# Cross-attention scores: the low 64 queries as one 64-row tile beside two groups of 32 high queries

## The chip, the core and the metric

The kernel runs on one core of a Trainium2 chip. The core has five engines with queues of their own: TensorE (PE in the profile; PEld are its weight loads), VectorE (DVE), ScalarE (ACT), GpSimd (POOL) and SyncE (SP, which issues most DMAs). The metric is the device time of one launch in microseconds, as the median of several runs. Before the change it is 1574.82 us (three runs, 1572.63 to 1575.15).

## What is computed

A block of cross-attention with a feed-forward network, in float32, for 128 sequences of 128 tokens with 256 features, 16 heads of 16 features. The part that matters here:

```python
q = (x @ Wq + bq).reshape(b, s, 16, 16).transpose(0, 2, 1, 3)
k = (ctx @ Wk + bk).reshape(b, s, 16, 16).transpose(0, 2, 1, 3)
v = (ctx @ Wv + bv).reshape(b, s, 16, 16).transpose(0, 2, 1, 3)
scores = jnp.einsum('bhqd,bhkd->bhqk', q, k) / 4.0
scores = jnp.where(j < i, scores, -1e30)       # query i sees the keys before it
attn = jax.nn.softmax(scores, axis=-1)
attn = attn.at[:, :, 0, :].set(0.0)
a = jnp.einsum('bhqk,bhkd->bhqd', attn, v).transpose(0, 2, 1, 3).reshape(b, s, 256)
x1 = layer_norm(x + a @ Wo + bo, ln1_g, ln1_b)
out = layer_norm(x1 + relu(x1 @ W1 + b1) @ W2 + b2, ln2_g, ln2_b)
```

The mask is causal: a query among the first 32 needs at most 32 keys, one among the first 64 at most 64, and so on.

## The kernel before

Two sequences are worked on together; there are 64 such pairs p. All orders are written by hand: the kernel turns the scheduler off (`manual_schedule`) for all five engines, so the text order of the calls is the order on each engine's queue. Pairs 0 and 1 are a start-up of their own (with `scores`, line 340, in which a tile is 32 rows by 64 queries); `third`, `fourth` and `fifth` are pairs 2 to 4; `step` (line 1227) is the regular step for p = 5 to 63, and `behind` (line 1303) finishes the last pairs. One step holds parts of several pairs: scores of p, context (`weigh`) and output projection of p - 2, hidden layer of p - 3, second FFN product of p - 4, and the projections for p + 1.

On TensorE a regular step is this row: `weigh(p-2)` (lines 572 and 583), `scores_both(p)` (line 412), `queries(p+1)` (271), `attention_out(p-2)` (603), `keys(p+1)` (271), `values(p)` (303), `second_by_seven(p-4)` (881), `hidden(p-3)` (790).

**Scores.** The 128 queries of a sequence fall into four groups of 32, g = 0 to 3, and group g is multiplied with its first `LENGTH[g]` = 32, 64, 96 or 128 keys. `group_scores` (line 402) makes one matmul for each chunk m of heads, sequence s and strip r of 32 rows: the stationary operand is 32 rows by 32 queries, the moving one 2 x `LENGTH[g]` columns (two heads), the output goes to the 32 PSUM partitions 32c with c = 2s + m, in a bank chosen by r. All four groups thus use 32x32 tiles of the array: 16 matmuls a group, 64 a step. `scores_both` (line 419) runs them in eight blocks of eight, alternating between strips 0, 1 and strips 2, 3.

**Softmax.** Groups 0 and 1 are called `LO`, groups 3 and 2 `HI`. For `LO`, DVE adds the mask from PSUM into the buffer `sm` (`masked`, line 432) and takes the maxima (`largest`, 439); ACT makes the exponentials head by head (`exponential_by_head`, 847), for `HI` straight out of PSUM; `divided` (455) sums on DVE, takes the reciprocal and multiplies on POOL (465); `turned` (485) transposes blocks of 32x32 on DVE into `tb`; `brought` (495) issues 16 DMAs on SP, which bring the pieces of `tb` to the partitions of `pT`, the moving operand of `weigh`. Two copies of `pT` alternate. Parts of it that no DMA writes are cleared once for each copy (`clear`, 369 and 370).

**Pads.** `empty(n)` (line 223) puts n NOP instructions into TensorE's queue. `second_by_seven` (872) computes the second FFN product as seven partial products of four matmuls each, with 11 or 10 pads spread over each product: 74 a step. `hidden` has three or four pads behind each matmul for p below 3. A float32 matmul call is four TensorE instructions (two weight loads and two matmuls), so a regular step has 172 calls, 74 pads and six waits: 768 instructions.

Of the kernel before, what the change touches and what calls it, by code (L numbers as in the profile page):

```python
# [19 lines left out]
def tile_cross_attention_block(  # L20
# [341 lines left out]
    for i in range(2):  # L362
        pT = const.tile([P, NS, 2, 12, 32], F32, tag=f"pT{i}", name=f"pT{i}")
        pTs.append(pT)

    def clear(p):

        pT = pTs[p % 2]
        nc.gpsimd.memset(pT[32:64, :, 0, 0:4, :], 0.0)
        nc.gpsimd.memset(pT[96:128, :, 0], 0.0)  # L370

    LENGTH = (32, 64, 96, 128)
    START = (2304, 1792, 1024, 0)
    COLUMN = (0, 384, 128, 512)
    WITHIN = (0, 32, 0, 96)
    HI, LO = (3, 2), (1, 0)

    def weights(p, g):

        st = states[p]  # L380
        if "sm" not in st:
            st["sm"] = wide(f"sm_{p}")
            st["nmx"] = small.tile([P, 4, HH], F32, tag="nmx", name=f"nmx_{p}")
            st["su"] = small.tile([P, 4, HH], F32, tag="su", name=f"su_{p}")
            st["rs"] = small.tile([P, 4, HH], F32, tag="rs", name=f"rs_{p}")
        n = LENGTH[g]
        return st["sm"][:, START[g] : START[g] + HH * n].rearrange("p (h j) -> p h j", j=n)

    def first_bank(p, g):
        return 4 if p > 3 and g < 2 else 0  # L390

    def place(g, r):
        return r if g > 1 else (r + 2) % 4

    def in_banks(p, g, at=slice(0, 4)):

        first = first_bank(p, g)
        return banks[:, first + at.start : first + at.stop].rearrange(
            "p r (e x) -> p (r e) x", e=2
        )[:, :, WITHIN[g] : WITHIN[g] + LENGTH[g]]  # L400

    def group_scores(p, g, strips=range(NS)):

        st = states[p]
        n = LENGTH[g]
        for m in range(KC):
            for s in range(2):
                c = 2 * s + m
                for r in strips:
                    strip, first = slice(32 * r, 32 * r + 32), s * P  # L410
                    out = banks[32 * c : 32 * c + 32, first_bank(p, g) + place(g, r)]
                    nc.tensor.matmul(  # L412
                        out.rearrange("p (e x) -> p e x", e=2)[:, :, WITHIN[g] : WITHIN[g] + n],
                        st["qT"][strip, m, first + 32 * g : first + 32 * g + 32],
                        st["kT"][strip, m, :, first : first + n],
                        start=True, stop=True,
                    )

    def scores_both(p):

        one, two = (0, 1), (2, 3)
        for strips, g in (
            (two, 1), (one, 3), (two, 0), (one, 2),
            (two, 3), (one, 1), (two, 2), (one, 0),
        ):
            group_scores(p, g, strips)

    def masked(p, g, at=slice(0, 4)):

        n = LENGTH[g]  # L430
        heads = slice(2 * at.start, 2 * at.stop)
        nc.vector.tensor_tensor(  # L432
            weights(p, g)[:, heads], in_banks(p, g, at),
            diag[:, None, P - n :].to_broadcast([P, 2 * (at.stop - at.start), n]), ALU.add,
        )

    def largest(p, g, src=None, heads=slice(0, HH)):
        src = weights(p, g) if src is None else src
        nc.vector.tensor_reduce(  # L439
            states[p]["nmx"][:, g, heads], src, AX.X, ALU.max, negate=True  # L440
        )

    def shifted(p, g):

        sm = weights(p, g)
        largest(p, g)
        nc.gpsimd.tensor_tensor(
            sm, sm, states[p]["nmx"][:, g, :, None].to_broadcast([P, HH, LENGTH[g]]), ALU.add
        )
# [5 lines left out]
    def divided(p, gs):  # L455

        st = states[p]
        su, rs = st["su"], st["rs"]
        for g in gs:
            nc.vector.tensor_reduce(su[:, g], weights(p, g), AX.X, ALU.add)  # L460
        part = slice(min(gs), max(gs) + 1)
        nc.vector.reciprocal(rs[:, part], su[:, part])
        for g in gs:
            sm = weights(p, g)
            nc.gpsimd.tensor_tensor(  # L465
                sm, sm, rs[:, g, :, None].to_broadcast([P, HH, LENGTH[g]]), ALU.mult
            )

    def turned(p, g):

        st = states[p]
        if "tb" not in st:
            st["tb"] = wide(f"tb_{p}").rearrange("p (j n) -> p j n", j=NS)
        tb, sm = st["tb"], weights(p, g)
        n = 128 if g < 2 else 256
        to = tb[:, :, COLUMN[g] : COLUMN[g] + n].rearrange("p j (n a) -> p n j a", a=32)
        if g == 0:
            to = to[:, :, 0::2]
            sm = sm.rearrange("p (r e) a -> p r e a", e=2)
        elif g == 1:  # L480
            sm = sm.rearrange("p (r e) (k a) -> p r (e k) a", e=2, a=32)
        else:
            to = to[:, :, : g + 1]
            sm = sm.rearrange("p h (j a) -> p h j a", a=32)
        nc.vector.transpose(to, sm)  # L485
# [75 lines left out]
    def weigh(p):  # L561
# [6 lines left out]
        for m in range(KC):  # L568
            for s in range(2):
                at = (m * 2 + s) * P  # L570
                for j in range(NS):
                    nc.tensor.matmul(  # L572
                        pc[32 * j : 32 * j + 32, at : at + HP],
                        st["vd"][:, s, 4 * m + j].rearrange("p e d -> p (e d)"),
                        pT[:, 2 * s + m, :, (j + 2) % 4, :] if new
                        else pT[:, 2 * s : 2 * s + 2, H + 2 * j + m, :],
                        start=True, stop=True,
                    )
            for s in range(2):
                at = (m * 2 + s) * P  # L580
                for e in range(2):
                    for j in range(NS):
                        nc.tensor.matmul(  # L583
                            pc[32 * j : 32 * j + 32, at + HP : at + P],
                            st["vz"][:, s, 4 * m + j, 2 * e : 2 * e + 2, :].rearrange(
                                "p e d -> p (e d)"
                            ),
                            pT[:, 2 * s + m, :, 4 + 2 * j + e, :] if new
                            else pT[:, 2 * s : 2 * s + 2, 4 * j + 2 * m + e, :],
                            start=(e == 0), stop=(e == 1),  # L590
                        )
# [187 lines left out]
    def hidden(p, fs, between=None):  # L779
# [3 lines left out]
        for f in fs[::2]:  # L783
# [4 lines left out]
            for i in range(2):  # L788
                for k in range(KC):
# [5 lines left out]
                    if p < 3:  # L795
                        empty(3 + (2 * f + 2 * i + k < 12))
# [42 lines left out]

    def exponential_by_head(p, gs, heads):  # L840

        st = states[p]
        for h in heads:
            for g in gs:
                sm = weights(p, g)
                src = in_banks(p, g)[:, h] if g > 1 else sm[:, h]
                nc.scalar.activation(  # L847
                    sm[:, h], src, AF.Exp, bias=st["nmx"][:, g, h : h + 1], scale=1.0
# [23 lines left out]
    def second_by_seven(p):  # L872
# [19 lines left out]
        product(py[:, :P], raw(0, 0), weights(0, 0), 11)  # L892
        product(pz[:, :P], raw(1, 0), weights(1, 0), 11)
        product(pz[:, 2 * P : 3 * P], raw(1, 1), lambda k: wt[:, 3, k], 11)
        product(py[:, 3 * P :], lambda k: hs[:, 0, k], lambda k: wt[:, 0, k], 11)
        product(py[:, 2 * P : 3 * P], lambda k: hs[:, 2, k], lambda k: wt[:, 2, k], 10)
        product(py[:, P : 2 * P], lambda k: hs[:, 1, k], lambda k: wt[:, 1, k], 10)
        product(pz[:, P : 2 * P], lambda k: hs[:, 3, k], weights(1, 1), 10)
# [36 lines left out]
    warm = bank("warm")  # L935
    for i in range(12):
# [135 lines left out]
    def low_scores(p):  # L1072
        for g in LO:
            group_scores(p, g)
# [7 lines left out]
    def third():  # L1082
# [20 lines left out]
        divided(p, (3,))  # L1103
# [6 lines left out]
        divided(p, (2,))  # L1110
# [3 lines left out]
        divided(p, LO)  # L1114
# [24 lines left out]
    def fourth():  # L1139
# [12 lines left out]
        divided(p, (3,))  # L1152
        powers(p, 2)
        second_sum(0)
        divided(p, (2,))
        weigh(p - 1)
        context(p - 1)
        for g in LO:
            group_scores(p, g)
# [15 lines left out]
        divided(p, LO)  # L1175
# [13 lines left out]
    def fifth():  # L1189
# [19 lines left out]
        divided(p, (3,))  # L1209
        for g in LO:  # L1210
            powers(p, g)
        divided(p, (2,))
        divided(p, LO)
# [5 lines left out]
        for g in (3, 2, 1, 0):  # L1219
# [7 lines left out]
    def step(p):  # L1227
# [23 lines left out]
        if p > 5:  # L1251
            exponential_by_head(p, LO, range(HH))
# [9 lines left out]
        if p == 5:  # L1262
            exponential_by_head(p, LO, range(HH))
# [4 lines left out]
        divided(p, (3,))  # L1268
        divided(p, (2,))
        divided(p, LO)  # L1270
# [15 lines left out]
        for g in (2, 1, 0):  # L1286
# [108 lines left out]
```

## Time and profile before

| | |
|---|---|
| median of three runs | 1574.82 us |
| the profiled execution | 1573.26 us, span of its instructions 1571.5 us |
| granted TensorE clock, mean | 0.998 |
| busy: PE, PEld, DVE, ACT, POOL | 98%, 88%, 77%, 69%, 78% |
| TensorE matmul records | 21894 |
| DMA engines, mean over the span | 120 GB/s |

The span goes from the first to the last instruction of the program. Starts of matmuls are observed; their ends are modelled, and matmuls are pipelined, so that the time between two starts says more than the length of a row. In the rows, "128*32 128x64 f32 x16" is a tile of 128 rows by 32 columns with 64 moving columns, 16 records; one matmul call leaves two records, one for each of its passes. NOPs stand under PEldq, the sequencer of TensorE.

### The profile page before, as it was taken

To read this page: it belongs to the slowest core of one execution; us is meant where nothing else is said; L and a number is where in the kernel's file an instruction comes from. 1 tells how busy PE (TensorE), PEld (TensorE's weight loads), DVE (VectorE), ACT (ScalarE), POOL (GpSimd) and SP (SyncE) were. 2 spreads that over 40 slices of the span, in tenths; PEclk is the share of its full clock that TensorE was granted. 3 is DMA by queue.
4 is the path that set the end of the run, shared out by engine and by line. 5 is a ranking of instruction groups with operands and counts; after the bars stand their busy time and mean duration, and the time that the engine had idled before them with its cause. 6 is when DMAs were issued, how large, how long until landed. Compare 5 with 4: busy or idle time off the path is not lost.

```text
span 1571.5 us, 59475 instructions
## 1 busy us (share of the span) xinstructions
PE 1545.9 (98%) x21894; PEld 1385.6 (88%) x21894; DVE 1208.4 (77%) x2548; ACT 1089.3 (69%) x3394; POOL 1226.3 (78%) x1364
## 2 busy tenths in 40 slices
PE   8998999999999999999999999999999999999997
PEld 6876989989989989899899899899899899899897
DVE  7876877778778778778778778778778787787764
ACT  5556767767767767767767677677677677677652
POOL 7865878887887788788788788788788778878874
PEclk9999999999999999999999999999999999999999
DMA  8445545545555555555455555455455455554331
GB/s 192 90 103 111 133 116 129 123 117 125 134 120 122 123 121 128 126 124 125 117 123 128 127 126 129 108 128 132 117 129 127 110 129 130 123 125 108 95 85 46
DMA packets 415329, 188.73 MB, mean 120 GB/s; under 512 B 282448, under 2 KB 390992, under 8 KB 415056
## 3 DMA queue, kind: packets, MB, share of 16 engines
q1 hardware_dynamic: 413152, 184.00, 50.9%
q8 instruction: 190, 3.11, 0.9%
q10 hardware_dynamic: 1904, 0.93, 0.3%
q14 instruction: 83, 0.68, 0.1%
HBM read 70.26 MB, written 33.29 MB: 66 GB/s over the span
## 4 chain that ended last, share of the span: by engine, by line
PE 94%; POOL 2%; DVE 2%; ACT 1%; DMA 1%; issue 1%; SPq 0%; ACTq 0%; POOLq 0%; DVEq 0%
PE banks L790 27%; PE banks L881 23%; PE banks L271 14%; PE banks L412 7%; PE banks L603 7%; PE banks L303 7%; PE banks L583 3%; PE banks L572 2%; PE banks L810 0%; ACT sm L847 0%; POOL sm L537 0%; DMA pT<-tb 0%; DMA c_first<-in_ctx_dram 0%; DMA x1T<-x1t 0%; PE banks L1346 0%
## 5 line engine op out<-in xcount | busy, mean ns | idle before, releaser
L790 PE MATMUL banks<-x1T,w 128*128 128x256 f32 x2048 | 453.9, 379 | 2.0 <-ACT kT L293 1.2
L790 PEld LDWEIGHTS banks<-x1T,w 128*128 128x128 f32 x2048 | 384.4, 190 | 53.0 <-ACT kT L293 1.6
L798 ACT ACTIVATE hT<-banks,b1e_c 128x256 f32<-128x256 f32 x504 | 211.2, 471 | 222.5 <-PE banks L790 222.3
L847 ACT ACTIVATE sm<-banks,nmx 128x128 f32<-128x128 f32 (+1 forms) x944 | 237.0, 402 | 154.4 <-POOL hS L869 141.8
L465 POOL TENSOR_TENSOR sm<-sm,rs 128x1024 f32<-128x1024 f32 x248 | 303.9, 1255 | 7.5 <-ACT vd L318 4.3
L432 DVE TENSOR_TENSOR sm<-banks,diag 128x256 f32<-128x256 f32 (+1 forms) x250 | 82.6, 371 | 211.4 <-PE banks L412 204.2
L623 POOL TENSOR_SCALAR ve<-mv 128x2 f32<-128x2 f32 x127 | 29.2, 230 | 250.9 <-DVE mv L617 250.4
L847 ACT ACTIVATE sm<-sm,nmx 128x64 f32<-128x64 f32 (+1 forms) x944 | 223.0, 422 | 0.0
L460 DVE TENSOR_REDUCE su<-sm 128x8 f32<-128x1024 f32 x248 | 192.3, 796 | 30.0 <-ACT sm L847 24.3
L485 DVE STREAM_TRANSPOSE tb<-sm 128x1024 f32<-128x1024 f32 x248 | 191.4, 811 | 0.2 <-POOL sm L465 0.2
L881 PE MATMUL banks<-wt,hS 128*128 128x128 f32 x1440 | 171.4, 275 | 2.2 <-POOL hS L868 2.2
L881 PEld LDWEIGHTS banks<-wt,hS 128*128 128x128 f32 x1440 | 165.9, 192 | 2.7 <-POOL hS L868 2.6
L439 DVE TENSOR_REDUCE nmx<-banks 128x4 f32<-128x512 f32 x236 | 136.3, 620 | 4.0
L412 PE MATMUL banks<-kT,qT 32*32 32x64 f32 (+3 forms) x7936 | 130.9, 305 | 2.3 <-issue 1.7
L271 PE MATMUL banks<-xT,wq 128*128 128x256 f32 x504 | 127.3, 396 | 3.5 <-DVE sm L432 3.5
L293 ACT ACTIVATE kT<-banks,bkh,half 128x256 f32<-128x256 f32 x252 | 125.5, 635 | 4.0 <-PE banks L271 3.9
L412 PEld LDWEIGHTS banks<-kT,qT 32*32 32x32 f32 x7936 | 108.8, 103 | 18.4 <-issue 3.5
L303 PE MATMUL banks<-wv,cT 128*128 128x256 f32 x512 | 121.1, 379 | 1.4 <-ACT sm L847 1.4
L603 PE MATMUL banks<-wo,cxT 128*128 128x256 f32 x512 | 122.0, 381 | 0.0
L271 PE MATMUL banks<-cT,wk 128*128 128x256 f32 x504 | 119.3, 379 | 1.6 <-DVE sm L432 1.6
L881 PEld LDWEIGHTS banks<-w,hT 128*128 128x128 f32 x960 | 116.5, 192 | 3.3
L881 PE MATMUL banks<-w,hT 128*128 128x128 f32 x960 | 117.2, 275 | 0.0
(137 smaller groups left out, 2916.9 us busy)
## 6 DMA issues: line engine op xcount, KB each, us to landing
pT<-tb SPq DMA_DIRECT2D x492, 96.0 KB, 2.2
pT<-tb SPq DMA_DIRECT2D x246, 80.0 KB, 2.1
x1t<-tbx SPq DMA_DIRECT2D x252, 64.0 KB, 3.1
x1T<-x1t SPq DMA_DIRECT2D x63, 256.0 KB, 2.8
out_dram<-t SPq DMA_DIRECT2D x63, 256.0 KB, 2.4
xb<-in_x_dram SPq DMA_DIRECT2D x124, 128.0 KB, 3.6
cb<-in_ctx_dram SPq DMA_DIRECT2D x124, 128.0 KB, 3.8
x<-in_x_dram SPq DMA_DIRECT2D x31, 512.0 KB, 4.8
```

What stands on the lines that cost most here:

```text
L271: nc.tensor.matmul(ps[:, m * TP : (m + 1) * TP], w[:, k, m * P : (m + 1) * P], src[:, k, :], start=(k == 0), stop=(k == KC - 1),)
L303: nc.tensor.matmul(pv[:, s * D : (s + 1) * D], st["cT"][:, k, s * P : (s + 1) * P], wv[:, k, :], start=(k == 0), stop=(k == KC - 1),)
L412: nc.tensor.matmul(out.rearrange("p (e x) -> p e x", e=2)[:, :, WITHIN[g] : WITHIN[g] + n], st["qT"][strip, m, first + 32 * g : first + 32 ...
L439: nc.vector.tensor_reduce(states[p]["nmx"][:, g, heads], src, AX.X, ALU.max, negate=True)
L460: nc.vector.tensor_reduce(su[:, g], weights(p, g), AX.X, ALU.add)
L465: nc.gpsimd.tensor_tensor(sm, sm, rs[:, g, :, None].to_broadcast([P, HH, LENGTH[g]]), ALU.mult)
L485: nc.vector.transpose(to, sm)
L603: nc.tensor.matmul(po[:, s * D : (s + 1) * D], cxT[:, k, s, :], wo[:, k, :], start=(k == 0), stop=(k == KC - 1),)
L790: nc.tensor.matmul(ph[:, i * TP : (i + 1) * TP].rearrange("p (s i a) -> p s i a", s=2, a=32), w1[:, k, (f + i) * P : (f + i + 1) * P], st[ ...
L798: nc.scalar.activation(st["hT"][:, f + i, :], ph[:, i * TP : (i + 1) * TP], AF.Relu, bias=(b1e_c if p else b1_c)[:, f + i : f + i + 1], sc ...
L847: nc.scalar.activation(sm[:, h], src, AF.Exp, bias=st["nmx"][:, g, h : h + 1], scale=1.0)
L881: nc.tensor.matmul(out, left(k), right(k), start=(k == 0), stop=(k == FC // 2 - 1))
```

## The change

The two low groups become one group of 64 queries with 64 keys. Its matmuls (`low_products`) have 32 rows by 64 queries as stationary operand and 2 x 64 moving columns, and write 64 PSUM partitions at once: 16 matmuls in place of 32, so 48 a step in place of 64. The high groups keep their 32x32 tiles. In `scores_both` the low matmuls go in four blocks of four between the high blocks. In the softmax the low group is now 16 heads of 64 keys for 64 queries of both sequences, 1024 elements in each partition where there were 512 and 256; each operation on it is one instruction in place of two, except the exponentials, which stay 16. The layout of `sm`, `tb` and `pT` changes with it, and the DMAs in `brought` with their sizes: 96 KB for j = 0 to 2, and 32 or 64 KB for j = 3, where there were 96, 80, 96 and 48. The masked-out piece of `pT` is cleared in one operation. The pads of `second_by_seven` become 20 or 19 a product, 138 a step, so that a regular step has 156 calls, 138 pads and six waits, again 768 instructions. The pads in `hidden` go.

```diff
-    LENGTH = (32, 64, 96, 128)
-    START = (2304, 1792, 1024, 0)
-    COLUMN = (0, 384, 128, 512)
-    WITHIN = (0, 32, 0, 96)
-    HI, LO = (3, 2), (1, 0)
+        nc.gpsimd.memset(pTs[p % 2][96:128], 0.0)
+    HEADS = (H, None, HH, HH)
+    LENGTH = (HP, None, 96, P)
+    START = (1792, None, 1024, 0)
+    WITHIN = (0, None, 0, 96)
+    COLUMN = (256, None, 0, 512)
...
+    def low_products(p, strips=range(NS), ms=range(KC)):
+        st = states[p]
+        bank0 = 4 if p > 3 else 0
+        for m in ms:
+            for s in range(2):
+                for r in strips:
+                    strip, first = slice(32 * r, 32 * r + 32), s * P
+                    nc.tensor.matmul(
+                        banks[s * HP : (s + 1) * HP, bank0 + (r + 2) % 4, m * P : (m + 1) * P].rearrange(
+                            "p (e j) -> p e j", e=2
+                        ),
+                        st["qT"][strip, m, first : first + HP],
+                        st["kT"][strip, m, :, first : first + HP],
+                        start=True, stop=True,
+                    )
...
     def scores_both(p):
         one, two = (0, 1), (2, 3)
-        for strips, g in (
-            (two, 1), (one, 3), (two, 0), (one, 2),
-            (two, 3), (one, 1), (two, 2), (one, 0),
-        ):
-            group_scores(p, g, strips)
+        low_products(p, two, (0,))
+        group_scores(p, 3, one)
+        low_products(p, two, (1,))
+        group_scores(p, 3, two)
+        group_scores(p, 2, one)
+        low_products(p, one, (0,))
+        group_scores(p, 2, two)
+        low_products(p, one, (1,))
...
-    def divided(p, gs):
+    def divided(p, g):
         st = states[p]
-        su, rs = st["su"], st["rs"]
-        for g in gs:
-            nc.vector.tensor_reduce(su[:, g], weights(p, g), AX.X, ALU.add)
-        part = slice(min(gs), max(gs) + 1)
-        nc.vector.reciprocal(rs[:, part], su[:, part])
-        for g in gs:
-            sm = weights(p, g)
-            nc.gpsimd.tensor_tensor(
-                sm, sm, rs[:, g, :, None].to_broadcast([P, HH, LENGTH[g]]), ALU.mult
-            )
+        sm = weights(p, g)
+        nc.vector.tensor_reduce(st["su"][g], sm, AX.X, ALU.add)
+        nc.vector.reciprocal(st["rs"][g], st["su"][g])
+        nc.gpsimd.tensor_tensor(sm, sm, per_head(p, g, "rs"), ALU.mult)
...
-            first = (0, 128, 0, 384)[j]
+            first = 0 if j < 3 else 256 if i % 2 else 512
...
-                        pT[:, 2 * s + m, :, (j + 2) % 4, :] if new
+                        pT[:, 2 * s : 2 * s + 2, 1, 2 * ((j + 2) % 4) + m, :] if new
...
-                            pT[:, 2 * s + m, :, 4 + 2 * j + e, :] if new
+                            pT[:, 2 * s + m, 0::2, 2 * j + e, :] if new
...
-                    if p < 3:
-                        empty(3 + (2 * f + 2 * i + k < 12))
...
-        product(py[:, :P], raw(0, 0), weights(0, 0), 11)
+        product(py[:, :P], raw(0, 0), weights(0, 0), 20)
...
-        product(pz[:, P : 2 * P], lambda k: hs[:, 3, k], weights(1, 1), 10)
+        product(pz[:, P : 2 * P], lambda k: hs[:, 3, k], weights(1, 1), 19)
...
-        for g in (2, 1, 0):
+        for g in (2, 0):
             turned(p, g)
```

In `step`, `fifth` and the others, loops over `LO` now have one group; `masked`, `largest`, `shifted`, `turned` and `exponential_by_head` take the new shapes at their old places.

More of the change, by code (lines that the diff above doesn't have):

```diff
@@ L382, in weights @@
             st["sm"] = wide(f"sm_{p}")
-            st["nmx"] = small.tile([P, 4, HH], F32, tag="nmx", name=f"nmx_{p}")
-            st["su"] = small.tile([P, 4, HH], F32, tag="su", name=f"su_{p}")
-            st["rs"] = small.tile([P, 4, HH], F32, tag="rs", name=f"rs_{p}")
+            for of in ("nmx", "su", "rs"):
+                t = small.tile([P, 2 * H], F32, tag=of, name=f"{of}_{p}")
+                st[of] = {3: t[:, :HH], 2: t[:, HH:H], 0: t[:, H:]}
         n = LENGTH[g]
[L387 to L393, printed above, removed]
-    def in_banks(p, g, at=slice(0, 4)):
[L397 to L400, printed above, removed]
+        return st["sm"][:, START[g] : START[g] + HEADS[g] * n].rearrange("p (h j) -> p h j", j=n)
+    def in_banks(p, g, at=slice(0, 4)):
+        if not g:
+            first = 4 if p > 3 else 0
+            return banks[:, first + at.start : first + at.stop, : 4 * HP].rearrange(
+                "p r (n j) -> p r n j", j=HP
+            )
+        return banks[:, at].rearrange("p r (e x) -> p (r e) x", e=2)[
+            :, :, WITHIN[g] : WITHIN[g] + LENGTH[g]
+        ]
     def group_scores(p, g, strips=range(NS)):
@@ L410, in group_scores @@
                     strip, first = slice(32 * r, 32 * r + 32), s * P
-                    out = banks[32 * c : 32 * c + 32, first_bank(p, g) + place(g, r)]
                     nc.tensor.matmul(
-                        out.rearrange("p (e x) -> p e x", e=2)[:, :, WITHIN[g] : WITHIN[g] + n],
+                        banks[32 * c : 32 * c + 32, r].rearrange("p (e x) -> p e x", e=2)[
+                            :, :, WITHIN[g] : WITHIN[g] + n
+                        ],
                         st["qT"][strip, m, first + 32 * g : first + 32 * g + 32],
@@ L428, in masked @@
     def masked(p, g, at=slice(0, 4)):
         n = LENGTH[g]
[L431 to L434, printed above, removed]
-        )
-    def largest(p, g, src=None, heads=slice(0, HH)):
+        k = HEADS[g] // 4
+        src = in_banks(p, g, at)
+        sm = weights(p, g)[:, k * at.start : k * at.stop]
+        if g:
+            no = diag[:, None, P - n :].to_broadcast([P, k * (at.stop - at.start), n])
+        else:
+            sm = sm.rearrange("p (r n) j -> p r n j", n=4)
+            no = neg[:, 1, None, None, :].to_broadcast([P, at.stop - at.start, 4, HP])
@@ L446, in shifted @@
         largest(p, g)
-        nc.gpsimd.tensor_tensor(
-            sm, sm, states[p]["nmx"][:, g, :, None].to_broadcast([P, HH, LENGTH[g]]), ALU.add
-        )
+        nc.gpsimd.tensor_tensor(sm, sm, per_head(p, g, "nmx"), ALU.add)
     def powers(p, g):
@@ L935, in tile_cross_attention_block @@
     warm = bank("warm")
+    empty(0)
     for i in range(12):
@@ L1072, in low_scores @@
     def low_scores(p):
-        for g in LO:
-            group_scores(p, g)
+        low_products(p)
         for g in LO:
@@ L1151, in fourth @@
         tokens(p + 2, "c")
-        divided(p, (3,))
+        divided(p, 3)
         powers(p, 2)
         second_sum(0)
-        divided(p, (2,))
+        divided(p, 2)
         weigh(p - 1)
         context(p - 1)
-        for g in LO:
-            group_scores(p, g)
+        low_products(p)
         scale_w1()
@@ L1218, in fifth @@
         combine_w2()
-        for g in (3, 2, 1, 0):
+        for g in (3, 2, 0):
             turned(p, g)
@@ L1251, in step @@
         if p > 5:
-            exponential_by_head(p, LO, range(HH))
+            exponential_by_head(p, LO, range(H))
         if not last:
@@ L1262, in step @@
         if p == 5:
-            exponential_by_head(p, LO, range(HH))
+            exponential_by_head(p, LO, range(H))
         values(p)
```

62 lines of the change are left out of this document (29 added, 33 removed).

## The prediction

> **What bounds the kernel now.** First the page's busy shares and its chain of waits.
>
> ```profile
> span 1571.5 us, 59475 instructions
> ...
> PE 1545.9 (98%) x21894; PEld 1385.6 (88%) x21894; DVE 1208.4 (77%) x2548; ACT 1089.3 (69%) x3394; POOL 1226.3 (78%) x1364
> ...
> PE 94%; POOL 2%; DVE 2%; ACT 1%; DMA 1%; issue 1%; SPq 0%; ACTq 0%; POOLq 0%; DVEq 0%
> PE banks L790 27%; PE banks L881 23%; PE banks L271 14%; PE banks L412 7%; PE banks L603 7%; PE banks L303 7%; PE banks L583 3%; PE banks L572 2%; PE banks L810 0%; ACT sm L847 0%; POOL sm L537 0%; DMA pT<-tb 0%; DMA c_first<-in_ctx_dram 0%; DMA x1T<-x1t 0%; PE banks L1346 0%
> ```
>
> TensorE (PE) is on 94% of the chain that ends last. A busy PE need not be at its peak, so next come two steps as windows (length, then busy time and instructions of PE, PEld, DVE, ACT, POOL), cut from one start of `weigh` to the next.
>
> ```profile
> 797.29:821.05 23.76, 23.76 (x346) 21.49 (x345) 18.70 (x40) 17.24 (x55) 18.96 (x22) 1.00 0.51 112
> 821.05:844.81 23.76, 23.76 (x346) 21.49 (x345) 18.70 (x40) 17.24 (x55) 18.98 (x22) 1.00 0.58 135
> ```
>
> The two steps are equal to 0.01 us, at granted clock 1.00, and PE is never idle in them; DVE, ACT and POOL have 4.8 to 6.5 us to spare. So what counts is how PE's own queue of work changes. The timeline of PE in the first of them:
>
> ```profile
> 797.29 0.43 PE L572 MATMUL banks<-pT,vd 128*32 128x64 f32 x16
> ...
> 798.78 2.07 PE L412 MATMUL banks<-kT,qT 32*32 32x128 f32 x128
> 800.78 1.99 PE L271 MATMUL banks<-xT,wq 128*128 128x256 f32 x8
> ...
> 804.34 1.89 PE L271 MATMUL banks<-cT,wk 128*128 128x256 f32 x8
> 806.07 1.89 PE L303 MATMUL banks<-wv,cT 128*128 128x256 f32 x8
> 807.79 1.95 PE L881 MATMUL banks<-w,hT 128*128 128x128 f32 x16
> ...
> 814.04 7.07 PE L790 MATMUL banks<-x1T,w 128*128 128x256 f32 x32
> ```
>
> Starts tell the cost: scores 800.78 - 798.78 = 2.00 us, second FFN product 814.04 - 807.79 = 6.25, hidden 821.05 - 814.04 = 7.01 (219 ns for each of 32 records of 256 columns, 0.85 ns a column). A matmul call of this kernel leaves two records here (two passes), so the 128 score records are 64 calls at 31 ns.
>
> **The change, part 1: score matmuls.** 32 calls on 32x32 tiles with 64 and 128 moving columns go; 16 on 32x64 tiles with 128 columns come; the 32 calls of the high groups stay. At 31 ns a call, 48 calls take 1.50 us: 0.50 us a step less. But the tiles are mixed: low, high 3, low, high 3 and 2, low, high 2, low: six changes between 32x64 and 32x32 inside `scores_both`, where there was none. What a change of tile shape costs stands in the timeline at three places.
>
> ```profile
> 820.74 0.38 PE L790 MATMUL banks<-x1T,w 128*128 128x256 f32 x1
> 821.05 0.24 PE L572 MATMUL banks<-pT,vd 128*32 128x64 f32 x1
> ...
> 15.41 0.38 PE L271 MATMUL banks<-xT,wq 128*128 128x256 f32 x1
> 15.72 0.69 PE L350 MATMUL banks<-kT,qT 32*64 32x128 f32 x32
> 16.34 0.48 PE L271 MATMUL banks<-cT,wk 128*128 128x256 f32 x1
> ...
> 9.97 1.34 PE L350 MATMUL banks<-kT,qT 32*64 32x256 f32 x32
> 11.24 0.33 PE L238 MATMUL banks<-ident,x 128*128 128x128 f32 x1
> ```
>
> From a 256-column pass to the next shape it is 0.31 us (821.05 - 820.74 and 15.72 - 15.41) instead of 0.22: some 0.09 us in which nothing streams, for 128x128 to 128x32 as for 128x128 to 32x64. The start-up's low scores are just the new form: 16 calls, each of the eight tiles with four passes of 128 columns, 4 x 0.11 = 0.44 us; they take 16.34 - 15.72 = 0.62, so a block between two changes costs 0.18 us above its passes.
>
> If each of the six changes drains PE, `scores_both` is a row of seven blocks, and each tile of a block has two passes: four low blocks of 0.22, high 3 alone 0.44, high 3 with high 2 on other rows 0.44 to 0.55, high 2 0.33, together 2.1 to 2.2 us, plus seven times 0.09 (the gap alone) to 0.18: 2.7 to 3.5 us. I take 3.2, by the 0.62-us row, since the short blocks cannot fill the wait for their second pass. That is +1.2 us a step; `scores_both` runs in 60 steps (4 to 63): +72 us. No row shows 32x64 next to 32x32, so without a drain the end on the other side is -0.5 x 60 = -30 us.
>
> [...]
>
> **Part 2: the pads.** `second_by_seven` gets 138 NOPs in place of 74: five for most calls instead of two or three. They fill no engine, but PE's sequencer. Its rows, in order: a stretch of 808.209 to 808.294; one of 808.222 to 808.280; one of 807.79 to 812.20; one of 804.30 to 807.79.
>
> ```profile
> L225 PEldq NOP  x2: 13/13/13, 808.2 to 808.3; - x2
> ...
> nothing on L225; most used: ['L881', 'L847', 'L460', 'L93', 'L668']
> ...
> L225 PEldq NOP  x52: 13/13/13, 807.8 to 812.1; - x52
> ...
> L225 PEldq NOP  x22: 13/13/13, 804.4 to 807.5; - x22
> ```
>
> Two NOPs lie inside 85 ns with 58 empty ns between them, so they start 71 or 72 ns apart. The 52 in 4.3 us hold 3.7 us; the rest over some 20 calls leaves at most 0.03 us for dispatching a call. The first NOP, behind the first call of the product, comes at 804.4, when PE starts `keys`: eight calls (`keys` and `values`) or 3.4 us ahead of that call on PE. The last comes at 812.1, with eight calls still to run (1.9 of 6.25 us). So the sequencer runs eight calls ahead, and the 74 pads just fit: a call and 2.64 pads, 0.22 us at most, beside 0.223 on PE.
>
> With five pads a call costs 5 x 71 + 20 to 30 = 0.38 us. Eight calls are issued when PE starts the product, 20 calls and 98 pads are not: 98 x 0.071 + 20 x 0.03 = 7.6 us against PE's 6.25. PE would run dry for 1.3 us in each of 57 steps (7 to 63), and in the two `behind` calls, where short `weigh` matmuls give no lead, for some 28 x 0.38 - 6.25 = 4.2 us each; with the last call +84 us in all. The pads become free where 98 x + 0.6 = 6.25: at 58 ns a NOP. In the profiled execution each NOP leaves a record, and its own row is 13 ns long; what it costs unprofiled lies between 13 and 71, and the trace cannot tell on which side of 58. I take the lower side for the forecast, by a little; the other is a rival.
>
> [...]
>
> The pads of the first three `hidden` go (180 NOPs), at most four beside a call of 0.44 us: hidden before, nothing won.
>
> **Part 3: the other engines.** One low group of 16x64 takes the place of 8x64 and 8x32.
>
> ```profile
> L465 POOL TENSOR_TENSOR sm<-sm,rs 128x1024 f32<-128x1024 f32 x62 | 117.6, 1896 | 1.4 <-DVE rs L462 1.3
> ...
> L465 POOL TENSOR_TENSOR sm<-sm,rs 128x512 f32<-128x512 f32 x62 | 64.6, 1042 | 4.7 <-ACT vd L318 4.3 <-DVE rs L462 0.4
> ...
> L465 POOL TENSOR_TENSOR sm<-sm,rs 128x256 f32<-128x256 f32 x62 | 38.1, 615 | 0.0
> ...
> L460 DVE TENSOR_REDUCE su<-sm 128x8 f32<-128x1024 f32 x62 | 73.6, 1188 | 1.3 <-ACT sm L453 1.3
> ...
> L460 DVE TENSOR_REDUCE su<-sm 128x8 f32<-128x512 f32 x62 | 42.4, 684 | 24.9 <-ACT sm L847 24.3 <-ACT sm L453 0.6
> ...
> L460 DVE TENSOR_REDUCE su<-sm 128x8 f32<-128x256 f32 x62 | 25.4, 409 | 0.0
> ...
> L847 ACT ACTIVATE sm<-sm,nmx 128x64 f32<-128x64 f32 x472 | 205.2, 437 | 0.0
> L847 ACT ACTIVATE sm<-sm,nmx 128x32 f32<-128x32 f32 x472 | 192.0, 407 | 0.0
> ...
> PE banks L572 <- DMA pT<-tb: 0.3, 1, 0.3
> ...
> pT<-tb SPq DMA_DIRECT2D x492, 96.0 KB, 2.2
> pT<-tb SPq DMA_DIRECT2D x246, 80.0 KB, 2.1
> ```
>
> POOL: 1896 - 1042 - 615 = +0.24 us a step. DVE: the sum 1188 - 684 - 409 = +0.10, about the same for the maximum and for the transpose, some -0.07 for the masks (two of 512 elements for four): about +0.3. ACT: 8 x 30 ns = +0.24. All of it lies in the 4.8 us and more that these engines have beside PE: nothing, unless that cover went. `brought` issues the same 16 transfers on SP, four of them 96 instead of 80 KB; PE waited for them 0.3 us in the whole run. The fifth score block writes banks 6 and 7 behind the `context` copy from bank 7, as before. Nothing.
>
> **Sum.** 1573.26 (the profiled execution's own time; span 1571.5, median of the runs 1574.82, so 1.6 us above it) + 72 = 1645 us.
>
> **The rivals.**
> - *Drains, and pads at 71 ns too:* 1645 + 84 = 1729 us. For it: the only price the trace has. Against it: 58 ns is enough to undo it.
> - *No drain, pads at 71 ns:* 1573 - 30 + 84 = 1627 us. For it: 32x64 and 32x32 both use 32 rows, and the blocks alternate between strips.
> - *No drain, pads hidden:* faster, 1573 - 30 = 1543 us. One mechanism: PE's scores go by calls, 48 instead of 64. It decides where the block falls under 2.00 us; even with the same overlap, 0.5 us over six changes means that a change must cost less than 0.08 us. Against it: every change of shape that I looked at cost 0.09.
> - *Drains partly covered:* 1.5 us plus six gaps of 0.09, up to half of the block sum: 2.0 to 2.6 us, 1575 to 1610 us, around the old time or somewhat slower.
>
> **How the numbers follow.** Forecast 0.36, drains and pads 0.28, pads alone 0.10, faster 0.13, partly covered 0.13. The point is the forecast's 1645. The range is 1565 to 1740: it holds the first three and the fifth, and leaves out the faster case and what lies beyond the bounds of the block sum. A measurement of this kernel can tell 0.2%, about 3 us, from no change. Faster by more: 0.13 and a little of the last case, 0.14; within: 0.03; slower: 0.83.
>
> **What would show it.** Right: in a step of the changed kernel `scores_both` takes about 3.2 us from its first record to `queries`, with a gap of about 0.09 us at each change of form. For the pads: the time from the first record of the product to the first of `hidden` is 6.25 us or near 7.6, with the PE sequencer's NOPs running up to its end; if profile and unprofiled time part by tens of us, the NOP's record is why. POOL, DVE and ACT gain 0.2 to 0.3 us a step and PE still never waits for them. Wrong: low and high records overlapping in time in one score block, or a step that ends on a wait for POOL or a DMA.

## The result and the profile after

| | before | after |
|---|---|---|
| median | 1574.78 us (four runs, 1572.63 to 1575.15) | 1749.84 us (four runs, 1748.55 to 1752.20) |
| profiled execution, its span | 1573.26, 1571.5 us | 1748.55, 1746.8 us |
| granted TensorE clock | 0.998 | 0.997 |

The ratio is 1.1116, 95% interval 1.1097 to 1.1136: 11.2% slower. The forecast was 1645 us, its range 1565 to 1740; the time lies above it. The page of the changed kernel:

```profile
span 1746.8 us, 58786 instructions
...
PE 1722.8 (99%) x19910; PEld 1419.0 (81%) x19910; DVE 1271.8 (73%) x2240; ACT 1103.6 (63%) x3391; POOL 1246.9 (71%) x1297
...
PE 95%; DVE 1%; POOL 1%; ACT 1%; DMA 1%; issue 0%; SPq 0%; POOLq 0%; ACTq 0%; DVEq 0%
PE banks L891 27%; PE banks L801 26%; PE banks L271 13%; PE banks L614 6%; PE banks L303 6%; PE banks L406 5%; PE banks L423 5%; PE banks L594 3%; PE banks L583 2%; PE banks L819 0%; ACT sm L857 0%; DMA pT<-tb 0%; POOL sm L548 0%; DVE nmx L459 0%; SPq L506 0%
```

TensorE is still the chain, now with 10% of it in scores (L406 and L423; 7% before, on L412) and 27% in the second product (L891; 23% on L881). Two steps as windows (length, then busy time of PE, PEld, DVE, ACT, POOL):

```profile
824.85:851.40 26.55, 26.55 (x313) 21.96 (x312) 19.73 (x35) 17.48 (x55) 19.27 (x20) 1.00 0.46 103
851.40:878.00 26.60, 26.60 (x313) 22.00 (x312) 19.76 (x35) 17.48 (x55) 19.26 (x20) 1.00 0.52 123
```

A step has 26.55 to 26.60 us where it had 23.76, again with PE never idle by the records. POOL gained 0.3 and ACT 0.24 us, about as forecast; DVE gained 1.03 us, where 0.3 was forecast. All three are further from the bound than before (6.8 us and more beside PE, where it was 4.8 and more). The timeline of PE in the first of these steps shows which blocks grew:

```profile
824.85 0.43 PE L583 MATMUL banks<-pT,vd 128*32 128x64 f32 x16
...
826.33 0.45 PE L423 MATMUL banks<-kT,qT 32*64 32x128 f32 x8
826.71 0.66 PE L406 MATMUL banks<-kT,qT 32*32 32x256 f32 x16
827.30 0.45 PE L423 MATMUL banks<-kT,qT 32*64 32x128 f32 x8
827.67 0.66 PE L406 MATMUL banks<-kT,qT 32*32 32x256 f32 x32
828.27 0.52 PE L423 MATMUL banks<-kT,qT 32*64 32x128 f32 x8
828.71 0.55 PE L406 MATMUL banks<-kT,qT 32*32 32x192 f32 x16
829.20 0.45 PE L423 MATMUL banks<-kT,qT 32*64 32x128 f32 x8
829.57 1.99 PE L271 MATMUL banks<-xT,wq 128*128 128x256 f32 x8
...
836.59 1.95 PE L891 MATMUL banks<-w,hT 128*128 128x128 f32 x16
838.37 1.06 PE L891 MATMUL banks<-wt,hT 128*128 128x128 f32 x8
839.26 3.65 PE L891 MATMUL banks<-wt,hS 128*128 128x128 f32 x24
842.75 1.61 PE L891 MATMUL banks<-w,hS 128*128 128x128 f32 x8
844.33 7.14 PE L801 MATMUL banks<-x1T,w 128*128 128x256 f32 x32
```

Read by starts, the score block falls apart into seven rows that never mix: 0.38, 0.59, 0.37, 0.60, 0.44, 0.49 and 0.37 us, together 829.57 - 826.33 = 3.24 (2.00 before). The single starts show the gaps between them: the last start of the first low row is at 826.51, its 128 columns take 0.11 us, and the first high start comes at 826.71, so that 0.09 us are empty, as at the changes of shape in the prediction. The second product takes 844.33 - 836.59 = 7.74 (6.25 before): its first 24 records keep the old pace (839.26 - 836.59 = 2.67 us, 0.22 a call), the last eight take 844.33 - 842.75 = 1.58, 0.40 a call. Start by start, calls 1 to 18 keep 0.22 us, and calls 19 to 28 take 0.30 to 0.42. The hidden layer takes 851.40 - 844.33 = 7.07 (7.01). Sum: 1.24 + 1.49 + 0.06 = 2.79 us, the whole difference of the steps. The NOPs of TensorE's sequencer, first from the start of the product to the hidden layer, then in the 3.5 us before it:

```profile
L225 PEldq NOP  x98: 13/13/13, 836.6 to 844.2; - x98
...
L225 PEldq NOP  x40: 13/13/13, 833.2 to 836.5; - x40
```

Forty pads are behind the sequencer when TensorE starts the product, and 98 fill it up to the end: 7.6 us.

### The profile page after: what moved, and what is told of

It reads as the page before. It is cut to its first block, busy times and chain, and to the rows that moved or that the text cites. A ratio compares the mean times of both kernels' runs of the same rounds, so it can differ in the third digit from the quotient of the medians.

```text
span 1746.8 us, 58786 instructions
## 1 busy us (share of the span) xinstructions
PE 1722.8 (99%) x19910; PEld 1419.0 (81%) x19910; DVE 1271.8 (73%) x2240; ACT 1103.6 (63%) x3391; POOL 1246.9 (71%) x1297
## 4 chain that ended last, share of the span: by engine, by line
PE 95%; DVE 1%; POOL 1%; ACT 1%; DMA 1%; issue 0%; SPq 0%; POOLq 0%; ACTq 0%; DVEq 0%
PE banks L891 27%; PE banks L801 26%; PE banks L271 13%; PE banks L614 6%; PE banks L303 6%; PE banks L406 5%; PE banks L423 5%; PE banks L594 3%; PE banks L583 2%; PE banks L819 0%; ACT sm L857 0%; DMA pT<-tb 0%; POOL sm L548 0%; DVE nmx L459 0%; SPq L506 0%
## 5 line engine op out<-in xcount | busy, mean ns | idle before, releaser
L482 POOL TENSOR_TENSOR sm<-sm,rs 128x1024 f32<-128x1024 f32 x186 | 321.9, 1758 | 7.7 <-ACT hT L807 4.9
L455 DVE TENSOR_TENSOR sm<-banks,neg 128x512 f32<-128x512 f32 (+1 forms) x122 | 84.8, 695 | 322.8 <-PE banks L423 322.8
L857 ACT ACTIVATE sm<-sm,nmx 128x64 f32<-128x64 f32 x944 | 235.4, 434 | 0.0
L480 DVE TENSOR_REDUCE su<-sm 128x8 f32<-128x1024 f32 x186 | 205.2, 1103 | 32.7 <-ACT sm L857 26.6
L891 PE MATMUL banks<-wt,hS 128*128 128x128 f32 x1440 | 225.8, 293 | 0.0
L891 PEld LDWEIGHTS banks<-wt,hS 128*128 128x128 f32 x1440 | 191.3, 190 | 29.6 <-issue 0.5
L496 DVE STREAM_TRANSPOSE tb<-sm 128x1024 f32<-128x1024 f32 x186 | 204.2, 1125 | 0.0
L877 POOL TENSOR_TENSOR hS<-hT 128x512 f32<-128x512 f32 x57 | 72.5, 1272 | 104.3 <-ACT hT L807 104.3
L891 PEld LDWEIGHTS banks<-w,hT 128*128 128x128 f32 x960 | 117.6, 192 | 4.6 <-issue 0.5
L891 PE MATMUL banks<-w,hT 128*128 128x128 f32 x960 | 119.5, 276 | 0.2
L406 PE MATMUL banks<-kT,qT 32*32 32x192 f32 (+1 forms) x3968 | 115.6, 360 | 0.6 <-ACT hT L807 0.6
```

What stands on the lines that cost most here:

```text
L406: nc.tensor.matmul(banks[32 * c : 32 * c + 32, r].rearrange("p (e x) -> p e x", e=2)[:, :, WITHIN[g] : WITHIN[g] + n], st["qT"][strip, m, ...
L480: nc.vector.tensor_reduce(st["su"][g], sm, AX.X, ALU.add)
L482: nc.gpsimd.tensor_tensor(sm, sm, per_head(p, g, "rs"), ALU.mult)
L857: nc.scalar.activation(sm[:, h], src, AF.Exp, bias=states[p]["nmx"][g][:, h : h + 1], scale=1.0)
L891: nc.tensor.matmul(out, left(k), right(k), start=(k == 0), stop=(k == FC // 2 - 1))
```

## The experiments

An experiment is one execution unless five rounds are named; the executions of one kernel lie within 3 to 6 us here.

**e1: the pads moved.** Theory: six changes of tile shape and 71 ns a pad, each for itself. Rivals: pads cost by number; the product is late for another reason.

```diff
-        product(py[:, :P], raw(0, 0), weights(0, 0), 20)
+        product(py[:, :P], raw(0, 0), weights(0, 0), 11)
...
         # in hidden, behind each matmul
+                    if p > 3:
+                        empty(4)
```

> The changed kernel with the pads moved: 74 in the second product as before the change (two or three behind a call), the other 64 in the hidden layer, four behind each call. Same 768 instructions and 138 pads a step, same scores. Theory (a NOP takes 71 ns of TensorE's sequencer, which runs eight calls ahead; five pads beside a 0.22-us call starve TensorE, four beside a 0.44-us call do not): the product is back at 6.25 us, the hidden layer at 7.00, scores stay at 3.25; a step of 24.99 us and some 1749.8 - 57 x 1.61 - 9 = 1649 us. Rival (pads cost by their number, wherever they stand): within 10 us of 1750. Rival (the product is late because the longer scores delay the sums on GpSimd): the product stays at 7.8 us, 1750.

Measured: 1649.14 us (before, on the same chip: 1574.22). Its timeline:

```profile
824.65 1.95 PE L893 MATMUL banks<-w,hT 128*128 128x128 f32 x16
...
830.90 7.07 PE L801 MATMUL banks<-x1T,w 128*128 128x256 f32 x32
837.90 0.43 PE L583 MATMUL banks<-pT,vd 128*32 128x64 f32 x16
```

The same 138 pads and 768 instructions: product 830.90 - 824.65 = 6.25, hidden 837.90 - 830.90 = 7.00. The scores stay at 3.25 us in the steps from 7 on. So 100.7 of the 175 us are pads that stand beside calls too short for them. A cost by number, and lateness of the sums on GpSimd, are out.

**e2: one tile shape.**

```diff
-                    nc.tensor.matmul(
-                        banks[s * HP : (s + 1) * HP, bank0 + (r + 2) % 4, m * P : (m + 1) * P].rearrange(
...
+                    for u in range(2):
+                        at = s * HP + 32 * u
+                        nc.tensor.matmul(
+                            banks[at : at + 32, bank0 + (r + 2) % 4, m * P : (m + 1) * P].rearrange(
...
+                            st["qT"][strip, m, first + 32 * u : first + 32 * u + 32],
```

(74 pads in the product; four behind each hidden call of pairs 0 to 2, which puts the regular steps at the same place against the 256-instruction pages as in the changed kernel. The pages are packets of TensorE's instruction queue: e4, with 3840 NOPs more than the kernel before, has 15 packets more, 205 against 190.)

> The changed kernel with each low matmul split into two 32x32 tiles (32 queries, the same 128 moving columns, the same PSUM places) in the same seven blocks; 74 pads in the second product, so again 768 instructions a step. Softmax, buffers and transfers stay those of the change. Theory (a change between 32x64 and 32x32 drains TensorE, and there are six of them): with one shape the blocks overlap again, 64 calls at 31 ns, scores about 2.0 us, and with the product at 6.25 some 1575 to 1585 us. Rival (the order of blocks or of strips, or the banks of the low scores, is what costs): scores stay above 3 us, some 1650 us.

Measured: 1588.61 us. The timeline of its score block (records of the low group on L425):

```profile
808.81 0.34 PE L425 MATMUL banks<-kT,qT 32*32 32x128 f32 x8
808.86 0.46 PE L406 MATMUL banks<-kT,qT 32*32 32x256 f32 x8
808.94 0.32 PE L425 MATMUL banks<-kT,qT 32*32 32x128 f32 x8
809.10 0.39 PE L406 MATMUL banks<-kT,qT 32*32 32x256 f32 x4
...
810.62 0.44 PE L425 MATMUL banks<-kT,qT 32*32 32x128 f32 x11
810.99 1.99 PE L271 MATMUL banks<-xT,wq 128*128 128x256 f32 x8
```

High records start 0.05 us behind the first low ones and both kinds alternate: 810.99 - 808.81 = 2.18 us for 64 calls where the 48 calls of mixed shape take 3.24. Order, banks and masks are the same. So 1.06 us a step, and 60.5 us against e1, come from the shapes. The time is 4 us above what was expected, as the scores take 2.18 us and not 2.0. The remaining 14 us over the kernel before are 0.18 us a step (the first 32 queries are now multiplied with 64 keys instead of 32, in another order; the two were not separated), some 11 us in 60 steps, and the start-up.

**e3: four pads a call.** 16 pads for each of the seven products, 26 in the hidden layer.

> The changed kernel with 112 pads in the second product (four behind each call) and 26 in the hidden layer; 768 instructions a step, scores as changed. Theory with the lead: 20 calls not yet issued when the product starts take 20 x (4 x 71 + 25) = 6.2 us, just the 6.25 that TensorE needs, so the product takes 6.25 to 6.4 us and the time is within 15 us of the kernel with 74 pads there (about 1650 to 1665). Theory without a lead (each call waits for its own pads): 28 x (0.31 - 0.22) = 2.4 us a step more, 1790 us. A price that is linear in the pads from 74 on: (112 - 74)/(138 - 74) of 1.6 us, 0.95 us a step, 1707 us.

Measured: 1671.13 us, 22.0 over e1. Its product and hidden layer:

```profile
807.21 1.95 PE L893 MATMUL banks<-w,hT 128*128 128x128 f32 x16
...
812.57 1.14 PE L893 MATMUL banks<-w,hS 128*128 128x128 f32 x8
813.65 7.14 PE L801 MATMUL banks<-x1T,w 128*128 128x256 f32 x32
```

813.65 - 807.21 = 6.44 us; in nearly every step 27 calls keep 0.22 us, and the last one takes some 0.4. The lead swallows most, not all: neither 2.4 us a step (no lead) nor 0.95 (linear) came, but 0.27 with the hidden layer, where I had allowed 0.15. That is 15.5 of the 22 us; 6 more lie in the last four products, behind the regular steps. The break-even lies just below four pads.

**e4: the pads in the kernel before.** `second_by_seven` of the kernel before with 20 and 19; 832 instructions a step.

> The kernel before the change, with nothing altered but the pads of the second product: 138 instead of 74, so 832 instructions a step. Theory: the pads alone cost 1.54 us a product and some 0.07 in the hidden layer, 57 x 1.61 + 9 = 101 us: 1676 us, scores still at 2.00. Rival (pads cost only together with the longer scores): 1575 to 1590.

Measured: 1733.54 us, 58 more than forecast. The product and the hidden layer are as in the changed kernel (medians of the steps 7.85 and 7.08 us there, 7.79 and 7.08 in the changed kernel), but some score blocks have a hole:

```profile
740.50 1.53 PE L412 MATMUL banks<-kT,qT 32*32 32x128 f32 x79
743.63 0.94 PE L412 MATMUL banks<-kT,qT 32*32 32x256 f32 x49 [1.60 <-issue]
744.50 2.08 PE L271 MATMUL banks<-xT,wq 128*128 128x256 f32 x4
...
PE banks L412 <- issue: 36.1, 30, 1.6
```

"issue" is time for which the profile shows nothing that was waited for; the last row, from the waits, counts 30 such holes (2 in the kernel before). Two of every four steps have one, and the place of a step against the 256-instruction pages repeats every four steps of 832.

**e5: 704 instructions.** The changed kernel with 74 pads in the product and none elsewhere.

> The changed kernel with the 74 pads of before in the second product and none elsewhere: 704 instructions a step, so that the boundaries of the 256-instruction pages, which TensorE's instruction DMA fetches, wander by 64 from step to step. Theory of drains and sequencer time alone: the same as with the other 64 pads in the hidden layer, 1649 us. Theory that a page boundary in the fast score blocks leaves TensorE without instructions, as two of every four steps showed with 832 instructions (one hole of 1.6 to 2.0 us in the scores): 1.6 to 2.0 us in a part of the 57 steps, 1675 to 1710 us.

Measured: 1656.47 us, 7.3 more than e1. Three steps of four take 24.99 us, as in e1, the fourth mostly 25.4 to 25.7. Neither figure came: there are holes here too, but few and short.

**e6, e7, e8: fewer changes.** Pads as in e1. e6 and e7 take the low matmuls first, then all high ones (one change of shape inside the block); e7 also puts the context product into bank 3; e8 has eight low, all high, eight low (two changes).

```diff
+        low_products(p, two)
+        low_products(p, one)
+        for g in HI:
+            for strips in (one, two):
+                group_scores(p, g, strips)
...
-        pc = at_bank(7, f"pc_{p}") if p > 1 else bank(f"pc_{p}")
+        pc = at_bank(3 if 1 < p < NP - 2 else 7, f"pc_{p}") if p > 1 else bank(f"pc_{p}")
```

> Pads as in the kernel with 64 of them in the hidden layer; the scores in two blocks: all 16 low matmuls, then all 32 of the high groups, so one change between 32x64 and 32x32 instead of six. Theory of drains: low 0.62 us as in the start-up, high 1.1 to 1.3, and, as the low strip 1 writes the bank that the context copy still reads until some 0.75 us after the first score, up to 0.7 us more: scores 1.8 to 2.6 us, 1562 to 1610 us. Rival (drains do not matter, low matmuls on 64 columns are slow in themselves): scores stay near 3.2 us, 1649.

> As the kernel with the low matmuls first, and the context product in bank 3 instead of bank 7, so that no low matmul waits for its copy. Theory of drains: scores 0.62 + 1.1 to 1.3, that is 1.7 to 1.95 us, and 1556 to 1571 us: 0.2 to 1.2% faster than the kernel before the change. Rival (the copy is not what holds the low block): no difference to the one with bank 7.

> Pads as in the kernel with 64 of them in the hidden layer; the scores in three blocks: eight low matmuls (strips 2 and 3), all high, eight low (strips 0 and 1): two changes instead of six, and no wait for the context copy. Theory of drains: 0.6 + 1.1 to 1.3 + 0.6 us, scores 2.3 to 2.5 us, 1592 to 1605 us. Rival: near 3.2 us, 1649.

Measured: e6 1617.70, e7 1582.25 (five rounds, ratio to before 1.0048, interval 1.0034 to 1.0062), e8 1606.13 us. Their score blocks, in this order:

```profile
797.79 1.48 PE L423 MATMUL banks<-kT,qT 32*64 32x128 f32 x32
799.19 1.39 PE L406 MATMUL banks<-kT,qT 32*32 32x256 f32 x64
800.51 0.70 PE L271 MATMUL banks<-xT,wq 128*128 128x256 f32 x2
```

```profile
810.18 0.72 PE L423 MATMUL banks<-kT,qT 32*64 32x128 f32 x32
810.83 1.42 PE L406 MATMUL banks<-kT,qT 32*32 32x256 f32 x64
812.17 1.99 PE L271 MATMUL banks<-xT,wq 128*128 128x256 f32 x8
```

```profile
816.39 0.67 PE L423 MATMUL banks<-kT,qT 32*64 32x128 f32 x16
816.99 1.41 PE L406 MATMUL banks<-kT,qT 32*32 32x256 f32 x64
818.33 0.67 PE L423 MATMUL banks<-kT,qT 32*64 32x128 f32 x16
818.92 1.99 PE L271 MATMUL banks<-xT,wq 128*128 128x256 f32 x8
```

Low matmuls on 64 columns are not slow in themselves: 16 of them take 0.65 us in e7. In e6 they take 1.40, as they wait for the copy from bank 7; e7 takes that wait away, 35 us. High takes 1.32 to 1.34 us, above what I had allowed (1.1 to 1.3), and all three times lie above what was expected of them, by 8, 11 and 1 us. e7's score block is 1.99 us, no better than before the change, and a gain did not come. Its steps are as short as before (23.74 us against 23.76), and what it loses is start-up: its step 6 starts at 138.95 us, in the kernel before at 127.55. Why is open.

**e9, e10: the high blocks in another order.** As e7, with the four high blocks as (one, 3), (two, 2), (two, 3), (one, 2) in e9 and (one, 3), (two, 2), (one, 2), (two, 3) in e10.

> As the kernel with the low matmuls first and the context product in bank 3, but the four high blocks alternate in length as well as in strips: high 3 on strips 0 and 1, high 2 on 2 and 3, high 3 on 2 and 3, high 2 on 0 and 1. The changed kernel's mixed block of 16 high calls took 0.60 us with the gap behind it, so two such blocks without a change between them should take some 1.1 us in place of 1.34: scores 1.75 us, a step of 23.5 us, 1563 to 1572 us, faster than the kernel before the change. Rival (32 high calls on 32x32 tiles take 1.34 us in any order): 1582 us.

> As the one with alternating high blocks, but high 2 of strips 0 and 1 third and high 3 of strips 2 and 3 last, so that the banks which are masked first are complete earlier. Theory that only the overlap of neighbouring blocks counts: as that kernel within 5 us. Rival (two blocks on other strips, then two on the same lengths, is no better than the plain order): 1582 us.

Measured: e9 1581.48 us (ratio 1.0040, 1.0026 to 1.0054), e10 1584.93 (1.0069, 1.0056 to 1.0082). In e9:

```profile
805.35 0.72 PE L423 MATMUL banks<-kT,qT 32*64 32x128 f32 x32
806.00 1.39 PE L406 MATMUL banks<-kT,qT 32*32 32x256 f32 x64
807.32 1.99 PE L271 MATMUL banks<-xT,wq 128*128 128x256 f32 x8
```

High takes 1.32 us, not 1.1: two mixed blocks in a row do not add up as one alone (0.60) suggested. The rival came. e9's steps of 23.71 us are the shortest of all, 0.03 below e7's and 0.05 below those of the kernel before; over 57 steps that is 3 us, and its start-up, 7.7 us longer, takes them back. e10 is within 5 us of e9, but slower. No version here beats the kernel before.

**e11, e12: the holes.** e11 is the kernel before with four more pads behind each hidden call from pair 4 on (832 instructions); e12 is the kernel before without the pads of pair 0 (768 instructions, 60 earlier against the pages).

> The kernel before the change with 64 more pads, four behind each call of the hidden layer from pair 4 on; the second product keeps its 74. 832 instructions a step as in the run with 138 pads in the product (1733.5 us). Theory that the pads of the product cost 1.6 us a step because they stand beside short calls, and that the rest of that run was holes in the scores from page boundaries: the product is back at 6.25 us, the hidden layer at 7.00, and what stays above 1575 us is the holes alone: up to 58 us, 1575 to 1633. Theory that the number of pads costs in itself: 1733.

> The kernel before the change without the 60 pads in the hidden layer of pair 0, nothing else: still 768 instructions a step, but every step stands 60 instructions earlier against the 256-instruction pages of TensorE's instruction DMA (its weigh starts 69 instead of 129 behind a boundary, which is near the place where the runs with 832 instructions had their holes). Theory that the place of the boundary decides about the holes: one hole in the scores of every step, 1.3 to 2.0 us in 57 steps, 1650 to 1690 us. Rival (the holes come from the wandering, not from the place): 1573 to 1580 us.

Measured: e11 1637.19 us; e12 1578.39, beside 1578.21 for the kernel before on that chip.

```profile
806.68 1.57 PE L412 MATMUL banks<-kT,qT 32*32 32x128 f32 x79
809.76 0.83 PE L412 MATMUL banks<-kT,qT 32*32 32x256 f32 x49 [1.50 <-issue]
810.52 1.99 PE L271 MATMUL banks<-xT,wq 128*128 128x256 f32 x8
...
817.53 1.95 PE L883 MATMUL banks<-w,hT 128*128 128x128 f32 x16
...
823.78 7.07 PE L790 MATMUL banks<-x1T,w 128*128 128x256 f32 x32
```

e11 has the product back at 823.78 - 817.53 = 6.25 us and keeps holes: 62 us above the kernel before, 4 more than expected. Added up over the regular steps by starts, 48 us of it are holes in the scores and 9 more are holes in `queries`, which a few of the same steps have. The same sums, with the last four products, give e4's 159 us as 106 of pads (101 forecast), 51 of holes and some start-up.

e12 did not try what it was meant to, for I had the place of the holes wrong. The table has the place of a step, that is, the number of TensorE's records ahead of it (weight loads, matmuls, NOPs, waits), counted from the place of the kernel before, modulo 256, and beside it the length of the score block in us (steps 7 to 62):

| place | kernel before, e12 | e4 | e11 |
|---|---|---|---|
| 0 | 2.00 to 2.06 (before) | 2.03 to 2.05 | 2.00 to 2.07 |
| 64 | | 3.05 to 3.74 | 2.95 to 3.96 |
| 128 | | 3.42 to 4.05 | 3.55 to 4.78 |
| 192 (e12: 196) | 2.00 to 2.15 (e12) | 2.00 to 2.12 | 2.00 to 2.12 |

All 28 steps of e4 at places 64 and 128 have a hole, and so have all 28 of e11; at 0 and 192 none has one. e12 stands at 196, beside a place without holes, so that its time fits both theories: it does not speak against the place. No kernel with every step at 64 or 128 was run.

## Why the prediction was wrong

**Mixed tile shapes: right, and to size.** 3.2 us forecast, 3.24 measured; 74 us instead of 72 over 60 steps. e2 shows the cause: the same blocks in one shape overlap and take 2.18. The sum by blocks held too: 2.1 to 2.2 us of passes leave about 0.15 us for each of the seven blocks, which is what nearly every block has above its passes. The after-trace agrees: no low record starts among high ones, and 0.09 us are empty at each of the six changes of the step shown.

**The pads: the step that failed.** The working gave +84 us at 71 ns a NOP, and then the forecast put the term at nothing: it took "the lower side" of 58 ns, because a NOP might be cheaper without its record. That was a guess with no row behind it. The 98 pads of the product fill 7.6 us, and moving them (e1) gives back 100.7 us. The profiled execution (1748.55 us) agrees with the other runs (1749.19 to 1752.20); whether a NOP's record is part of the 71 ns stays open, but the measured time has the 71 ns in it.

The first rival of the list, drains and pads at 71 ns, 1729 us, was the case that came. It is 21 us low. All products together became 97 us longer where it allowed 84: a regular one takes 7.74 to 7.82 us rather than 7.6, and that of step 63, which has no `keys` in front of it, 9.21; for the two in `behind` it had 4.2 us each, where its own 28 x 0.38 - 6.25 is 4.4, and they became 4.1 and 3.5 us longer. The hidden layer takes 0.07 us more in each step, which the rival left out: its first record lasts 0.29 us to the next start in place of 0.22. The rest is start-up: step 6 starts 4.6 us later.

**The price by calls: not borne out.** The cases without drains took 31 ns for each score call, 1.50 us for 48. The 32 high calls alone take 1.32 us (e9), 41 ns a call, and with one change of shape in place of six (e7) the block takes 1.99 us. Counted in moving columns of both passes, the score block before has 20480 in 2.00 us, that of e2 22528 in 2.18 and the high calls of e9 14336 in 1.32: 0.098, 0.097 and 0.092 ns a column (the mixed high block of the changed kernel, 7168 columns in 0.60 us, has 0.084). So the columns fit these blocks better than the calls do; no run separates the two by itself.

**The lead: right.** The sequencer runs eight calls ahead: forty pads were issued at the product's start, 98 were not, as worked out. The pace breaks when the lead is used up: with eight calls in hand and 0.38 us against 0.22 a call that is after some 19 calls, and in the trace the nineteenth is the first late one. e3 finds the break-even at just under four pads a call.

**The other engines: nothing on the path, as forecast; DVE was mis-sized.** POOL +0.24 us, as this group of the changed kernel shows (1901 against 1042 + 615 ns). DVE's durations grew by 0.4 us a step, about as forecast, but its busy time by 1.03 (18.70 to 19.73): fewer of its instructions overlap, 1.2 us a step (durations of 20.97 us) instead of 1.9 (20.57). The forecast had added up durations.

```profile
L482 POOL TENSOR_TENSOR sm<-sm,rs 128x1024 f32<-128x1024 f32 x124 | 235.7, 1901 | 6.8 <-ACT hT L807 4.9 <-DVE rs L481 1.9
```

**The range was too narrow at the top.** Its own terms reach above it: scores of 3.5 us (+90) with the pads (+84) make 1747 us, yet it ended at 1740. And the price of the pads stopped at 7.6 us a product, without the hidden layer and the start-up.

## What to carry to other kernels

Where TensorE is the bound, count its tile shapes as well as its calls: sixteen calls fewer cost 1.24 us a step because they were of another shape and stood between others. An instruction that does nothing still takes its turn on the sequencer, 71 ns here; put fillers beside calls long enough to cover them (here a call of 0.44 us covers four; a call of 0.22 us covers 2.64, and with a lead of eight calls nearly four over a product of 28). And where the trace has one price for a thing, forecast with it: a cheaper price that no row shows belongs to a rival.

## What was not expected of the hardware

- Steps of 832 instructions had a hole of 0.9 to 2.8 us in the scores in two of four steps (e4, e11), steps of 704 one of 0.4 to 0.75 us in most fourth steps (e5: 10 of 14), and steps of 768 none above 0.15 us at the places tried. In e4 and e11 the holes follow the place of the step (the table at e12). Why two places of four have them is open, and so is whether a kernel that keeps one of these places has a hole in every step.
- The 32 high calls take 1.32 to 1.34 us in a block of their own (41 ns a call); with low calls of the same shape and fewer columns among them a call takes 31 ns on average (64 in 2.00 us, the kernel before). The other order tried, e10, was slower: 2.07 us for the score block against 1.97 in e9.

The pages of 256 instructions are these packets of TensorE's instruction queue (number, MB, share; the kernel before, then e4):

```profile
q8 instruction: 190, 3.11, 0.9%
...
q8 instruction: 205, 3.36, 0.9%
```

e4 has 3840 NOPs more and 15 packets more: 256 instructions a packet, three packets in a step of 768. The totals agree: TensorE's matmuls, weight loads and NOPs, without its waits, are 2 x 21894 + 4620 = 48408 in the kernel before and 2 x 19910 + 8280 = 48100 in the changed one, which has 189 packets: 255 a packet in both. A score block of 64 calls is 256 instructions long, so every such block has a page boundary in it; a boundary there is not enough for a hole.
